# Two half buffers for the next layer's table, a group's later steps planned ahead of attention, and group buffers three deep

## The chip, the cores and the metric

The kernel runs on one core of a Trainium2 chip. Its time is the device time of one launch in microseconds (us). Three runs of the kernel before gave 5804.15, 5805.21 and 5806.6 us; their median, 5805.21 us, is the time before.

## The reference, cut to what matters

Two layers of a graph network with typed attention run over 6250 nodes of 128 values, 200,000 edges sorted by target node, 16 node types and 32 edge types; a linear map, the residual sum and a layer norm follow.

```python
def gt_layer(x, ntype, etype, src, dst, ...):          # H = 8 heads of 16, RT = 32 edge types
    k, q, v = (typed_linear(x, ntype, W) for W in (Wk, Wq, Wv))     # a matrix per node type
    kT = einsum('nhd,htdo->nhto', k, Watt)             # per node: 32 edge types x 128 values
    vT = einsum('nhd,htdo->nhto', v, Wmsg)
    a = einsum('ehd,ehd->eh', kT[src, :, etype], q[dst]) * pri[:, etype].T / sqrt(16)
    att = edge_softmax(a, dst, n)
    hag = segment_sum(vT[src, :, etype] * att, dst)
    h = silu(typed_linear(hag, ntype, Wa))
    h = h * alpha + x * (1 - alpha)                    # alpha: sigmoid(skip[ntype])
    return layernorm(h) * g + b
h = gt_layer(gt_layer(x, layer 0), layer 1)
out = layernorm(x + h @ ff_w + ff_b)
```

## The kernel before, in words

The nodes stand in 49 tiles of 128, ordered by their number of edges, so that a tile needs as many steps as its fullest node has edges, by a fixed table: 61 for the first tile, 45 for the next, down to 25, 24, 24 and 23 for the last four, 1613 in all. For each layer a table in DRAM holds, for each node and edge type, the row kT and vT (256 numbers, 1 KB). One step of a tile is one indirect DMA, issued by POOL (line 833), that gathers 128 such rows into a slot of the tile `ring` (64 slots in layer 0, 96 in layer 1).

There are three stages. First the edges are prepared and the table of layer 0 is written from x. Then layer 0 runs: POOL gathers, and VectorE (DVE) does attention over the slots (lines 854 to 888): scores, a softmax over the tile's steps, then the weighted values; a slot comes free only after its values are summed. Tiles form 15 groups, ten of four tiles and then groups of 3, 2, 2, 1 and 1. When a group's attention is done, `behind` takes it on: transposes of `hag` (line 384), sixteen masked matmuls with Wa (masks on DVE, line 937; matmuls, line 945), silu, the mixture with x, the norm; then `project` with another sixteen masks and three matmuls per mask for k, v and q of the next layer. A lock "m" lets one group at a time use these steps' PSUM banks; it is handed on when q is copied (line 952 or 954). Then `next_tables` computes, tile by tile, the rows of the next layer's table: 16 matmuls of 512 columns (line 442), each result copied by ScalarE (ACT) or DVE (line 451) into the staging tile `st`, 128 x 32 KB, and one indirect DMA of POOL (line 1049, 4 MB) that scatters `st` to the nodes' places. `st` is one buffer: a tile's copies wait for the landing of the tile before. Last comes layer 1: the same attention and `behind`, with `head` in place of `project`; its results are scattered to the output by line 1080.

The order of all instructions is made when the program is built, by a planner (`Plan`). Each step states its engine, its assumed duration and what it needs; the planner always takes the step that can start earliest, and among equals the one of the lower rank in RANK (attention 1, a group's later steps 3, table steps 0). Every engine then executes its list strictly in that order, so that an instruction that waits holds up all behind it on its engine. In the list a scatter stands MARGIN = 8 us behind the planned end of its copies, except in the last two groups. The planner knows nothing of a limit that the DMAs of POOL have in the trace.

Of the kernel before, what the change touches and what calls it, by code (L numbers as in the profile page):

```python
# [31 lines left out]
F32 = mybir.dt.float32  # L32
# [6 lines left out]
P = 128  # L39
# [21 lines left out]
RANK = dict(table=0, empty=0, gather=1, attend=1, prepare=2, mask=3, typed=3, late=4, query=1)  # L61
PLAN_US = None
GATHER_US = 1.31
# [36 lines left out]

class Clock:
# [24 lines left out]
class Plan:  # L126
# [3 lines left out]
    def __init__(self, us=0.0):  # L130
        self.free = {e: us for e in ("PE", "DVE", "ACT", "POOL", "SP", "DMA")}
        self.threads, self.born = [], 0
        self.clock = Clock()

# [12 lines left out]
    def start(self, t):  # L147
# [7 lines left out]
        if isinstance(took, Work):  # L155
            us = max(us, self.free["PE"])
            return None, us, "PE"
        names = engines if isinstance(engines, tuple) else (engines,)
# [3 lines left out]
    def run(self):  # L162
        while self.threads:
# [9 lines left out]
            if e == "PE":  # L173
                self.free[e], end, state = self.clock.run(us, t[4][1])
                self.clock.window, self.clock.busy, self.clock.full = state
            else:
                self.free[e] = end
            end += HOP_US
# [27 lines left out]
def gnn_kernel(ctx: ExitStack, tc: tile.TileContext, x, src, dst, etype, ntype, Wk, Wq, Wv, Wa,  # L206
# [221 lines left out]
    def table_rows(banks, st, kT, vT, j, bk, bv, needs, free):  # L428
# [3 lines left out]
        per = TAB // width  # L432
        halves = [[], []]
        for t0 in range(0, RT, per):
            i = 2 * t0 // RT
            filled = halves[i]
            for kv, (cT, blk) in enumerate(((kT, bk), (vT, bv))):
                for g in range(P // width):
# [10 lines left out]
                    def empty(to=st[:, t0 : t0 + per, c0 : c0 + width], tab=tab, done=done, us=us, i=i):  # L449
# [330 lines left out]
    def first_tables():  # L780
        free = [0.0, 0.0]
        for i, g in enumerate(GROUPS):
            yield "SP", 0.0, [made[i]]
            kT, vT = columns[i]
            for j, t in enumerate(g):
                dest = tables[0][t * P * RT : (t + 1) * P * RT].rearrange("(p t) c -> p t c", t=RT)
                halves = yield from table_rows(tabs, st, kT, vT, j, bk, bv, [made[i]], free)
# [39 lines left out]
    low = ctile("low", [P, NTILE, 2], I32)  # L827
    bp = ctx.enter_context(tc.tile_pool(name="bp", bufs=2))
# [99 lines left out]
    def typed_cols(fp, xm_bufs, xT, types, M, maps, needs):  # L928
# [11 lines left out]
        plan.spawn(mask(), RANK["mask"])  # L940
# [100 lines left out]
    def next_tables(i, kT, vT, bk, bv, us, at):  # L1041
        by_node = tables[1].rearrange("(n t) c -> n (t c)", t=RT)
        turn = locks["s"].take()
        for j, t in enumerate(LAST[i]):
            halves = yield from table_rows(tabs, at["rows"], kT, vT, j, bk, bv, [us, turn], [at["st"]] * 2)
            at["read"][i].us = plan.free["PE"] if j == len(LAST[i]) - 1 else None
            us = yield "SP", 0.0, halves[0] + halves[1]
            us = yield "POOL", GATHER_US, [us + (MARGIN if i + 2 < NG else 0.0)]
            s = nc.gpsimd.indirect_dma_start(
                out=by_node, out_offset=bass.IndirectOffsetOnAxis(ap=rec[:, t, 2:3], axis=0),  # L1050
                in_=at["rows"].rearrange("p t c -> p (t c)"), in_offset=None, bounds_check=NP - 1, oob_is_err=False)
            apart(s, "by_node")
            at["st"] = us + 16.0
        locks["s"].give(us - MARGIN)

    def head(fp, i, h, needs, at):
# [21 lines left out]
        for j, t in enumerate(g):  # L1078
            us = yield "POOL", GATHER_US, [us]
# [25 lines left out]
    def gathers(layer, ring, size, landed, freed):  # L1105
        for s in range(SLOTS):
            us = yield "POOL", GATHER_US, [freed[s - size]] if s >= size else []
# [4 lines left out]
    def attends(fp, layer, ring, pieces, st, weights, wa, landed, freed):  # L1112
        at = {c: [When() for _ in LAST] for c in ("hag", "h", "read", "out", "z", "ty")}
        at["st"], at["rows"] = 0.0, st
# [21 lines left out]
        for i, g in enumerate(LAST):  # L1136
            if i > 1:
                yield "SP", 0.0, [at["hag"][i - 2]]
            n = len(g)
            hag = fp.tile([P, GT, P], F32, tag="hag", name="hag", bufs=2)  # L1140
            for j, t in enumerate(g):
# [4 lines left out]
                if j == n - 1:  # L1146
                    got = yield "SP", 0.9, [at["ty"][i - 2]] if i > 1 else ()
                    xs = load4(fp, "xs", hid if layer else xperm, g[0], n, 2)
                    types = fp.tile([P, GT * P], F32, tag="types", name="types", bufs=2)
# [12 lines left out]
            plan.spawn(behind(fp, layer, i, hag, (xs, types, got + 3.0), [us], weights, wa, at), RANK["typed"], us)  # L1162

    for layer in range(L):
        last = layer == L - 1
        with tc.tile_pool(name=f"wp{layer}", bufs=1) as wp, tc.tile_pool(name=f"fp{layer}", bufs=1) as fp, \
# [8 lines left out]
            st = None if last else wp.tile([P, RT, ROW], F32, tag="st", name="st")  # L1175
# [136 lines left out]
```

## Time and profile before

| what | value |
|---|---|
| median of three runs | 5805.21 us |
| profiled execution | 5804.55 us, its span 5802.8 us |
| VectorE busy | 3647.5 us (63%) |
| POOL busy | 3589.4 us (62%), of it 3229.8 us in 3226 gathers |
| TensorE matmuls | 2683.0 us (46%), mean granted clock 0.674 |
| ScalarE busy | 908.2 us (16%) |

The span is the time from the first to the last instruction; the execution is 1.75 us longer. Times in the rows below count from the span's start. POOL's busy time covers the issue of a DMA, not its transfer.

### The profile page before, as it was taken

Reading aid. Unit: us, or ns where it says so; the run is one execution under the profiler, and the core shown is the slowest. Engines: PE = TensorE matmul, PEld = TensorE weight load, DVE = VectorE, ACT = ScalarE, POOL = GpSimd, SP = SyncE. Lnnn points to the kernel's source line nnn. Section 1 sums busy time; section 2 is a strip of 40 time slices with the busy share of each in tenths; the row PEclk is TensorE's granted clock in tenths of the full one; section 3 lists DMA queues with packets and bytes.
Section 4 is the critical chain, followed back from the end, with each engine's and each line's share of the span. In section 5 each row is a group of like instructions: output and inputs, shape, how many; then the busy total and the mean of one; then the engine's idle time right before and its main releaser. Section 6 shows DMA issues by size and latency. Waiting matters only on the chain. (4 is left out here: it accounts for less than half of the span.)

```text
span 5802.8 us, 36552 instructions
## 1 busy us (share of the span) xinstructions
PE 2683.0 (46%) x9472; PEld 1435.8 (25%) x9474; DVE 3647.5 (63%) x4965; ACT 908.2 (16%) x1768; POOL 3589.4 (62%) x3592
## 2 busy tenths in 40 slices
PE   5999998004656556676767785010111011111122
PEld 3666665002222222232223353000000000000011
DVE  5644453467667766676767551575676667766776
ACT  1333332001111121222212221000000000000001
POOL 2223511677777777767776602777777777777775
PEclk9999998556566667776677676555555555555555
DMA  7667766434545555555565534333333333333332
GB/s 207 244 247 271 280 237 265 107 102 133 183 161 188 181 185 174 194 190 189 189 209 193 193 129 155 107 109 102 106 109 108 102 106 110 108 108 107 106 108 71
DMA packets 331281, 924.13 MB, mean 159 GB/s; under 512 B 96992, under 2 KB 184412, under 8 KB 299704
## 3 DMA queue, kind: packets, MB, share of 16 engines
q0 software_dynamic: 172944, 649.13, 34.7%
q1 hardware_dynamic: 158120, 272.60, 13.2%
q8 instruction: 75, 1.23, 0.1%
q14 instruction: 142, 1.16, 0.1%
HBM read 485.42 MB, written 436.08 MB: 159 GB/s over the span
## 5 line engine op out<-in xcount | busy, mean ns | idle before, releaser
L833 POOL DMA_INDIRECT ring<-table,idx_all x3226 | 3229.8, 1001 | 1179.2 <-issue 997.3
L854 DVE TENSOR_TENSOR ring<-ring,sb 128x2048 f32<-128x2048 f32 (+13 forms) x261 | 453.8, 1739 | 889.9 <-DMA ring<-table,idx_all 877.3
L384 PE MATMUL xb<-ident,hag 128*128 128x128 f32 x98 | 39.8, 454 | 1826.0 <-DVE hag L1160 1824.0
L451 ACT COPY st<-tab 128x512 f32<-128x512 f32 x1165 | 628.1, 590 | 1198.6 <-PE tab L442 863.9
L885 DVE TENSOR_REDUCE add<-ring 128x128 f32<-128x2048 f32 (+13 forms) x269 | 735.5, 2734 | 9.1
L442 PE MATMUL tab<-bk,kT 32*128 32x512 f32 x1568 | 587.4, 784 | 330.9 <-ACT st L451 265.4
L442 PE MATMUL tab<-bv,vT 32*128 32x512 f32 x1568 | 577.4, 819 | 61.6 <-DVE st L451 34.2
L937 DVE SCALAR_TENSOR_TENSOR xm<-types,xb 128x512 f32<-128x512 f32 (+3 forms) x720 | 391.2, 584 | 241.8 <-PE aq L945 210.9
L945 PE MATMUL aq<-xm,wa 128*128 128x512 f32 (+3 forms) x960 | 448.0, 629 | 177.8 <-DVE xm L937 177.8
L856 DVE TENSOR_REDUCE sb<-ring 128x128 f32<-128x2048 f32 (+13 forms) x269 | 473.5, 1760 | 9.2
L384 PEld LDWEIGHTS xb<-ident,hag 128*128 128x128 f32 x98 | 17.9, 199 | 1861.0 <-DVE hag L1160 1842.5
L881 DVE TENSOR_TENSOR ring<-ring,sb 128x2048 f32<-128x2048 f32 (+13 forms) x269 | 469.4, 1745 | 0.0
L451 DVE COPY st<-tab 128x512 f32<-128x512 f32 x403 | 266.9, 686 | 218.7 <-PE tab L442 164.2
L1090 ACT COPY sb<-qr 128x128 f32<-128x128 f32 x96 | 25.9, 269 | 2099.7 <-DVE sb L856 1931.0
L945 PEld LDWEIGHTS aq<-xm,wa 128*128 128x128 f32 x960 | 208.4, 239 | 410.0 <-DVE xm L937 238.6
L397 DVE SCALAR_TENSOR_TENSOR xm<-types,xb 128x256 f32<-128x256 f32 (+1 forms) x400 | 157.5, 412 | 242.4 <-PE aq L414 241.2
L442 PEld LDWEIGHTS tab<-bk,kT 32*128 32x128 f32 x1568 | 183.4, 218 | 490.0 <-ACT st L451 359.5
L945 PE MATMUL ak<-xm,wk 128*128 128x512 f32 (+3 forms) x480 | 243.0, 591 | 107.2 <-DVE xm L937 107.1
L412 PE MATMUL kv<-xm,wk 128*128 128x256 f32 (+1 forms) x800 | 262.7, 410 | 9.2 <-DVE xm L397 9.2
L442 PEld LDWEIGHTS tab<-bv,vT 32*128 32x128 f32 x1568 | 193.5, 227 | 258.6 <-ACT st L451 162.5
L384 PE MATMUL xb<-ident,h 128*128 128x128 f32 x98 | 28.8, 437 | 493.6 <-DVE h L1011 493.6
L414 PEld LDWEIGHTS aq<-wq,xm 128*128 128x128 f32 x1568 | 238.7, 193 | 20.6
(176 smaller groups left out, 3105.1 us busy)
## 6 DMA issues: line engine op xcount, KB each, us to landing
table<-st SPq DMA_DIRECT2D x196, 1024.0 KB
ring<-table,idx_all POOLq DMA_INDIRECT x3226
state<-init SPq DMA_DIRECT2D x2, 3528.0 KB
state<-state SPq DMA_DIRECT2D x98, 72.0 KB
qr<-qrows SPq DMA_DIRECT2D x20, 256.0 KB
types<-tyrow SPq DMA_DIRECT2D x20, 256.0 KB
rows<-in_x_dram SPq DMA_DIRECT2D x24, 128.0 KB
types_i<-in_node_type_dram SPq DMA_DIRECT2D x24, 128.0 KB
```

Source lines behind the costliest of these rows:

```text
L397: nc.vector.scalar_tensor_tensor(xm, types[:, :M], float(t), xT[:, :M], op0=ALU.is_equal, op1=ALU.mult)
L412: nc.tensor.matmul(to, w[:, t], xm, start=False, stop=last_of)
L414: nc.tensor.matmul(to, xm[:, c], w[:, t], start=False, stop=last_of)
L442: nc.tensor.matmul(tab, cT[rows, nodes], blk[rows, t0 : t0 + per].rearrange("p t o -> p (t o)"), start=True, stop=True)
L451: (nc.scalar.copy if e == "ACT" else nc.vector.tensor_copy)(to, tab.rearrange("p (t o) -> p t o", o=width))
L833: nc.gpsimd.indirect_dma_start(out=ring[:, place], out_offset=None, in_=tables[layer], in_offset=bass.IndirectOffsetOnAxis(ap=idx[:, s : s ...
L854: nc.vector.tensor_tensor(kk, kk, q[:, None, :].to_broadcast([P, m, P]), op=ALU.mult)
L856: nc.vector.tensor_reduce(sc[:, s0 : s0 + m], kk.rearrange("p s (h d) -> p s h d", h=H), axis=AX.X, op=ALU.add)
L881: nc.vector.tensor_tensor(vv.rearrange("p s (h d) -> p s h d", h=H), vv.rearrange("p s (h d) -> p s h d", h=H), sc[:, s0 : s0 + m, :, None ...
L885: nc.vector.tensor_reduce(add, vv.rearrange("p s c -> p c s"), axis=AX.X, op=ALU.add)
L937: nc.vector.scalar_tensor_tensor(xm[:, :M], types[:, :M], float(t), xT[:, :M], op0=ALU.is_equal, op1=ALU.mult)
L945: nc.tensor.matmul(to[:, :M], w[:, t], xm[:, :M], start=(t == 0), stop=(t == NT - 1))
```

## The change

Four things change in the two layers; the preparation keeps its code.

`st` becomes two tiles of half the size, one for edge types 0 to 15 and one for 16 to 31. `next_tables` no longer waits with a tile for the landing of the one before: each half waits only for the scatter of the same half. Each half is scattered by a DMA of its own (`scatter`, 2 MB, POOL), by row numbers 2n and 2n + 1 in a new tile `half` (two small DVE instructions). The planner takes a half's landing to be 7.5 us after its issue, where it took 16 us for the whole.

The ranks change: a group's later steps get 1.2 and their masks 1.4, attention 1.6. Where both could start at once, the later steps now come first.

`hag`, `xs` and `types`, of which each group has one, are three deep, where they were two.

The planner gets a rule for POOL: a DMA may be issued only when the one issued eight before has landed (2.8 us for a gather, 8.0 us for a half scatter, as it assumes). A gather's issue is put at 1.303 us, where it was 1.31.

```diff
-RANK = dict(table=0, empty=0, gather=1, attend=1, prepare=2, mask=3, typed=3, late=4, query=1)
+RANK = dict(table=0, empty=0, gather=1, attend=1.6, prepare=2, mask=3, typed=3, late=4, query=1, behind=1.2, masks=1.4)
 PLAN_US = None
-GATHER_US = 1.31
+GATHER_US = 1.303
+LANES = 8
+LANDS_US = 2.8
+STORE_US = 8.0
...
+class Issue:
+    def __init__(self, us, lands):
+        self.us, self.lands = us, lands
...
+        if isinstance(took, Issue):
+            us = max(us, self.free["POOL"], self.lanes[-LANES])
+            return us + took.us, us, "POOL"
...
+                if isinstance(t[4][1], Issue):
+                    self.lanes.append(us + t[4][1].lands)
...
-                    def empty(to=st[:, t0 : t0 + per, c0 : c0 + width], tab=tab, done=done, us=us, i=i):
+                    def empty(to=st[i][:, :, c0 : c0 + width], tab=tab, done=done, us=us, i=i):
...
+    half = ctile("half", [P, NTILE, 2], I32)
+    for c in range(2):
+        nc.vector.tensor_scalar(half[:, :, c], rec[:, :, 2], 2.0, float(c), op0=ALU.mult, op1=ALU.add)
...
-        plan.spawn(mask(), RANK["mask"])
+        plan.spawn(mask(), RANK["masks"])
...
     def next_tables(i, kT, vT, bk, bv, us, at):
-        by_node = tables[1].rearrange("(n t) c -> n (t c)", t=RT)
         turn = locks["s"].take()
         for j, t in enumerate(LAST[i]):
-            halves = yield from table_rows(tabs, at["rows"], kT, vT, j, bk, bv, [us, turn], [at["st"]] * 2)
-            at["read"][i].us = plan.free["PE"] if j == len(LAST[i]) - 1 else None
-            us = yield "SP", 0.0, halves[0] + halves[1]
-            us = yield "POOL", GATHER_US, [us + (MARGIN if i + 2 < NG else 0.0)]
-            s = nc.gpsimd.indirect_dma_start(
-                out=by_node, out_offset=bass.IndirectOffsetOnAxis(ap=rec[:, t, 2:3], axis=0),
-                in_=at["rows"].rearrange("p t c -> p (t c)"), in_offset=None, bounds_check=NP - 1, oob_is_err=False)
-            apart(s, "by_node")
-            at["st"] = us + 16.0
-        locks["s"].give(us - MARGIN)
+            free, at["st"] = at["st"], [When(), When()]
+            halves = yield from table_rows(tabs, at["rows"], kT, vT, j, bk, bv, [us, turn], free)
+            for c in range(2):
+                plan.spawn(scatter(t, c, at["rows"][c], halves[c], at["st"][c], MARGIN if i + 2 < NG else 0.0, at),
+                           RANK["table"])
+        at["read"][i].us = plan.free["PE"]
+        locks["s"].give(plan.free["PE"])
+
+    def scatter(t, c, rows, filled, done, margin, at):
+        us = yield "SP", 0.0, filled
+        us = yield "POOL", Issue(GATHER_US, STORE_US), [us + margin]
+        s = nc.gpsimd.indirect_dma_start(
+            out=tables[1].rearrange("(n t) c -> n (t c)", t=RT // 2),
+            out_offset=bass.IndirectOffsetOnAxis(ap=half[:, t, c : c + 1], axis=0),
+            in_=rows.rearrange("p t c -> p (t c)"), in_offset=None, bounds_check=2 * NP - 1, oob_is_err=False)
+        apart(s, "by_node")
+        done.us = at["dma"] = max(us, at["dma"]) + 7.5
...
-            hag = fp.tile([P, GT, P], F32, tag="hag", name="hag", bufs=2)
+            hag = fp.tile([P, GT, P], F32, tag="hag", name="hag", bufs=3)
...
-            plan.spawn(behind(fp, layer, i, hag, (xs, types, got + 3.0), [us], weights, wa, at), RANK["typed"], us)
+            plan.spawn(behind(fp, layer, i, hag, (xs, types, got + 3.0), [us], weights, wa, at), RANK["behind"], us)
...
-            st = None if last else wp.tile([P, RT, ROW], F32, tag="st", name="st")
+            st = None if last else [wp.tile([P, RT // 2, ROW], F32, tag=f"st{c}", name=f"st{c}") for c in range(2)]
```

What this makes of the order is seen on two engines. POOL, layer 0, where the first scatters stand among the gathers, before (table_60 is the table of layer 0, table_61 that of layer 1):

```order
L833 DMA ring<-table_60,idx_all 128x256 x324
L1049 DMA table_61<-st,rec 6272x8192
L833 DMA ring<-table_60,idx_all 128x256 x30
L1049 DMA table_61<-st,rec 6272x8192
L833 DMA ring<-table_60,idx_all 128x256 x30
```

The same place now (st_6545 is the first half, st_6546 the second):

```order
L853 DMA ring<-table_60,idx_all 128x256 x286
L1075 DMA table_61<-st_6545,half 12544x4096
L853 DMA ring<-table_60,idx_all 128x256 x5
L1075 DMA table_61<-st_6546,half 12544x4096
L853 DMA ring<-table_60,idx_all 128x256 x12
```

The first scatter stands 38 gathers earlier, and the tiles of a group follow each other after 17 gathers and two scatters, where it was 30 gathers and one. POOL at the end of layer 0, before:

```order
L1049 DMA table_61<-st,rec 6272x8192
L833 DMA ring<-table_60,idx_all 128x256 x30
L1049 DMA table_61<-st,rec 6272x8192
L833 DMA ring<-table_60,idx_all 128x256 x8
L1049 DMA table_61<-st,rec 6272x8192 x9
L894 TENSOR_LOAD n_over
```

And now; of the ten scatters in a row at the end the first three are shown:

```order
L853 DMA ring<-table_60,idx_all 128x256 x4
L1075 DMA table_61<-st_6546,half 12544x4096
L853 DMA ring<-table_60,idx_all 128x256 x13
L1075 DMA table_61<-st_6545,half 12544x4096
L1075 DMA table_61<-st_6546,half 12544x4096
L1075 DMA table_61<-st_6545,half 12544x4096
```

Nine whole tiles stood behind the last gather, and 40 ahead of it; now five tiles (ten halves) stand behind it, and 88 halves ahead. DVE, layer 0, the ninth tile's softmax and first values (sb holds the scores, xm are masks of the group before, line 937), before:

```order
L865 TENSOR_TENSOR sb<-sb,top 128x312
L1006 SCALAR_TENSOR_TENSOR h<-h,al_87,xs 128x128 x2
L870 TENSOR_REDUCE den<-sb 128x8
L871 TENSOR_TENSOR state<-state,sb 128x8
L872 TENSOR_TENSOR den<-den,state 128x8
L873 TENSOR_TENSOR hag<-state,sb 128x128
L881 TENSOR_TENSOR ring<-ring,sb 128x16x128
L885 TENSOR_REDUCE add<-ring 128x128
```

The same place now:

```order
L885 TENSOR_TENSOR sb<-sb,top 128x312
L957 SCALAR_TENSOR_TENSOR xm<-types,xb 128x512 x4
L890 TENSOR_REDUCE den<-sb 128x8
L891 TENSOR_TENSOR state<-state,sb 128x8
L892 TENSOR_TENSOR den<-den,state 128x8
L893 TENSOR_TENSOR hag<-state,sb 128x128
L901 TENSOR_TENSOR ring<-ring,sb 128x16x128
L905 TENSOR_REDUCE add<-ring 128x128
L957 SCALAR_TENSOR_TENSOR xm<-types,xb 128x512 x2
L908 TENSOR_TENSOR hag<-hag,add 128x128
```

Masks of the projection, which stood behind this tile, now stand inside its attention, ahead of the sums that free ring slots.

## Rows read from the trace of the kernel before

**Rows 1.** Page: its head, its costliest group (busy, mean | idle).

```profile
span 5802.8 us, 36552 instructions
L833 POOL DMA_INDIRECT ring<-table,idx_all x3226 | 3229.8, 1001 | 1179.2 <-issue 997.3
```

**Rows 2.** Busy time by stage (instructions), granted clock, DMA share.

```profile
core 0: us, PE busy (x) PEld busy (x) DVE busy (x) ACT busy (x) POOL busy (x), PEclk, DMA share, GB/s
1001.34:3313.50 2312.16, 1277.07 (x2900) 543.43 (x2900) 1555.73 (x1855) 409.09 (x794) 1653.71 (x1653) 0.66 0.53 174
3313.50:3585.49 271.99, 216.72 (x784) 133.31 (x784) 112.31 (x242) 75.56 (x141) 9.74 (x11) 0.68 0.35 146
3585.49:5802.80 2217.31, 287.73 (x725) 150.76 (x725) 1489.57 (x1887) 124.82 (x259) 1665.05 (x1662) 0.54 0.36 105
```

**Rows 3.** Timeline, POOL, one scatter: start, us, instruction [idle, releaser].

```profile
1700.13 1.01 POOL L1049 DMA_INDIRECT table<-st,rec  x1 [0.30 <-issue]
1701.44 1.03 POOL L833 DMA_INDIRECT ring<-table,idx_all  x1 [0.30 <-issue]
...
1713.93 1.00 POOL L833 DMA_INDIRECT ring<-table,idx_all  x1 [3.63 <-DMA table<-st,rec]
1715.23 1.00 POOL L833 DMA_INDIRECT ring<-table,idx_all  x1 [0.31 <-issue]
```

**Rows 4.** Waits of POOL, 1001.34 to 3314: total, times, longest.

```profile
POOL ring L833 <- DMA table<-st,rec: 145.4, 39, 4.7
POOL ring L833 <- DVE add L885: 14.4, 4, 13.5
...
POOL table L1049 <- ACT st L451: 2.4, 2, 1.3
```

**Rows 5.** Groups by line, 1001.34 to 3313.5: busy, mean | idle.

```profile
L451 ACT COPY st<-tab 128x512 f32<-128x512 f32 x565 | 304.7, 589 | 587.3 <-PE tab L442 373.0 <-DMA table<-st,rec 213.6
...
L854 DVE TENSOR_TENSOR ring<-ring,sb 128x2048 f32<-128x2048 f32 (+14 forms) x129 | 220.3, 1708 | 369.4 <-DMA ring<-table,idx_all 365.7 <-DVE xm L937 0.8
```

**Rows 6.** Timeline, POOL, last gather of layer 0 to layer 1.

```profile
3313.50 0.99 POOL L833 DMA_INDIRECT ring<-table,idx_all  x1 [3.61 <-DMA table<-st,rec]
3328.48 1.01 POOL L1049 DMA_INDIRECT table<-st,rec  x1 [13.99 <-ACT st L451]
...
3457.67 0.96 POOL L1049 DMA_INDIRECT table<-st,rec  x1 [38.26 <-ACT st L451]
...
3568.75 0.96 POOL L1049 DMA_INDIRECT table<-st,rec  x1 [23.46 <-ACTq L896]
3585.49 1.05 POOL L833 DMA_INDIRECT ring<-table,idx_all  x1 [15.77 <-issue]
```

**Rows 7.** By stretch: the last scatter's transfer, the restart.

```profile
3570.35:3580.35 10.00, 0.00 (x0) 0.00 (x0) 0.00 (x0) 0.00 (x0) 0.00 (x0) 0.50 0.91 390
3580.35:3585.49 5.14, 0.00 (x0) 0.00 (x0) 0.00 (x0) 1.28 (x1) 0.01 (x1) 0.50 0.01 2
```

**Rows 8.** Timeline, DVE, end of the 47th tile's attention.

```profile
3274.08 0.29 DVE L1160 TENSOR_TENSOR hag<-hag,den 128x128 f32<-128x128 f32 x1
```

**Rows 9.** Timeline, TensorE, where two late groups take the lock.

```profile
3392.64 0.69 PE L384 MATMUL xb<-ident,hag 128*128 128x128 f32 x2 [0.46 <-ACT q L952]
...
3458.11 0.47 PE L384 MATMUL xb<-ident,hag 128*128 128x128 f32 x1 [0.46 <-ACT q L952]
```

**Rows 10.** Waits, 3313.5 to 3585.49: total, times, longest.

```profile
ACT st L451 <- DMA table<-st,rec: 110.2, 8, 29.4
```

**Rows 11.** Timeline, ScalarE, copies for the 47th and 48th tile.

```profile
3497.06 1.07 ACT L451 COPY st<-tab 128x512 f32<-128x512 f32 x2 [13.98 <-DMA table<-st,rec]
...
3524.80 0.58 ACT L451 COPY st<-tab 128x512 f32<-128x512 f32 x1 [6.38 <-DMA table<-st,rec]
```

**Rows 12.** Timeline, POOL, last gather and last output of layer 1.

```profile
5750.95 0.99 POOL L833 DMA_INDIRECT ring<-table,idx_all  x1 [0.30 <-issue]
...
5794.43 0.96 POOL L1080 DMA_INDIRECT out_dram<-o,rec  x1 [7.70 <-DVE o L976]
```

More of the change, by code (lines that the diff above doesn't have):

```diff
@@ L133, in __init__ @@
         self.clock = Clock()
+        self.lanes = [0.0] * LANES
     def spawn(self, steps, rank, us=0.0):
@@ L432, in table_rows @@
         per = TAB // width
+        assert 2 * per == RT
         halves = [[], []]
@@ L786, in first_tables @@
                 dest = tables[0][t * P * RT : (t + 1) * P * RT].rearrange("(p t) c -> p t c", t=RT)
-                halves = yield from table_rows(tabs, st, kT, vT, j, bk, bv, [made[i]], free)
+                halves = yield from table_rows(tabs, [st[:, : RT // 2], st[:, RT // 2 :]], kT, vT, j, bk, bv, [made[i]], free)
                 free = [When(), When()]
@@ L1078, in head @@
         for j, t in enumerate(g):
-            us = yield "POOL", GATHER_US, [us]
+            us = yield "POOL", Issue(GATHER_US, LANDS_US), [us]
             s = nc.gpsimd.indirect_dma_start(
@@ L1106, in gathers @@
         for s in range(SLOTS):
-            us = yield "POOL", GATHER_US, [freed[s - size]] if s >= size else []
+            us = yield "POOL", Issue(GATHER_US, LANDS_US), [freed[s - size]] if s >= size else []
             gather(layer, ring, idx_all, s, s % size)
@@ L1113, in attends @@
         at = {c: [When() for _ in LAST] for c in ("hag", "h", "read", "out", "z", "ty")}
-        at["st"], at["rows"] = 0.0, st
+        at["st"], at["rows"], at["dma"] = [0.0, 0.0], st, 0.0
         qs, ready, read = {}, [When() for _ in range(NTILE)], [When() for _ in range(NTILE)]
@@ L1136, in attends @@
         for i, g in enumerate(LAST):
-            if i > 1:
-                yield "SP", 0.0, [at["hag"][i - 2]]
+            if i > 2:
+                yield "SP", 0.0, [at["hag"][i - 3]]
             n = len(g)
-            hag = fp.tile([P, GT, P], F32, tag="hag", name="hag", bufs=2)
+            hag = fp.tile([P, GT, P], F32, tag="hag", name="hag", bufs=3)
             for j, t in enumerate(g):
@@ L1146, in attends @@
                 if j == n - 1:
-                    got = yield "SP", 0.9, [at["ty"][i - 2]] if i > 1 else ()
-                    xs = load4(fp, "xs", hid if layer else xperm, g[0], n, 2)
-                    types = fp.tile([P, GT * P], F32, tag="types", name="types", bufs=2)
+                    got = yield "SP", 0.9, [at["ty"][i - 3]] if i > 2 else ()
+                    xs = load4(fp, "xs", hid if layer else xperm, g[0], n, 3)
+                    types = fp.tile([P, GT * P], F32, tag="types", name="types", bufs=3)
                     nc.sync.dma_start(out=types[:, : n * P], in_=tyrow[ds(g[0] * P, n * P)][None, :].to_broadcast([P, n * P]))
```

## The prediction, made before the changed kernel was run

> **What bounds the kernel now.** I read the page first, then busy time by stage, then the waits and the timeline of POOL in layer 0, then the end of layer 0. The page shows no engine over 63% busy; the costliest group is POOL's gather, 3226 times [rows 1]. The span splits into a preparation up to 1001.3, the gathers of layer 0 (2312.2 us), the end of layer 0 without a gather (272.0) and layer 1 (2217.3) [rows 2]. In steady work one gather follows another after 1715.23 - 1713.93 = 1.30 us (1.303 over longer stretches) [rows 3], though one is busy for 1001 ns only [rows 1]. In layer 0 POOL issues 1613 gathers and 40 scatters up to the last gather, 1652 steps of 1.303 us = 2152.6 of the 2312.2 us. So issue by POOL bounds this stage; DVE is no bound, it stands 365.7 us before the scores waiting for gathers [rows 5].
>
> The other 159.6 us have two known causes. The first is a wait behind each scatter: seven gathers go out at the usual pace, and the eighth, due at 1710.6, starts at 1713.93, held until the scatter has landed [rows 3]. POOL's queue here takes eight DMAs in flight. 39 such waits are booked as 145.4 us [rows 4]; without the ordinary 0.30 us each they are 133.7, and a 40th of 3.8 us is booked on another line, so 137.5. The second is a wait of 13.1 us (13.45 less the ordinary gap; it is most of the 14.4) near the start, where the ring is full with the first tile [rows 4]. 9.0 us remain in small pieces.
>
> The end of layer 0 is the next place to look: 272 us in which POOL only issues the last nine scatters [rows 6]. ScalarE stands 110.2 us in it for the landing of a scatter before it may refill `st` [rows 10]. Layer 1 is bound by issue in the same way, but has no scatter of table rows: 1613 gathers and 45 output scatters by 1.303 us fill 2160 us of it up to the last gather [rows 2, 12].
>
> **The change, part by part.** The sum is made against the profiled execution, 5804.55 us, which is 0.66 us under the median of the three runs; its span is 5802.8 [rows 1], and 1.75 us lie around it.
>
> 1. Half scatters, the waits behind them. From issue to landing a scatter takes 13.7 us among gathers (the eighth gather starts 1713.93 - 1700.13 = 13.8 after it, less its own start) [rows 3], and 11.8 alone: of the 16.74 us from the last scatter to the restart, 5.1 belong to the restart [rows 6, 7]. Its transfer fills the DMA engines to 0.91 for 10.0 of those us [rows 7], so the time goes with the bytes. Half the bytes save 5: 8.7 us among gathers, 6.9 alone. The eighth DMA behind it is due after 8 x 1.303 = 10.4 us, so it no longer waits: -137.5 us. The bounds are 0 wait, and 3.4 us for each half if the landing didn't shrink.
>
> The Trainium skill, "DMA: Bandwidth & Descriptors", section "Anatomy of one DMA — SWDGE (gpsimd) path", puts a DMA of this kind at about 2.0 us plus its bytes by 436 GB/s, and its section "Rules for kernel authors" advises to join transfers into few large ones, which speaks against splitting. By that fit a whole scatter is 11.6 us, which the trace bears out with 11.8, and a half 6.8; the second fixed part, 49 x 2.0 = 98 us, would come on top if it stood on the path. Here POOL goes on issuing in that time, so I don't charge it.
>
> 2. Half scatters, the issue. 98 take the place of 49. By the order 88 stand ahead of the last gather where 40 stood: 48 x 1.303 = +62.5 us, all on the path, since POOL is the bound there.
>
> 3. POOL waits for its own scatters' data. Before, 40 scatters waited 2.4 us in all [rows 4]. But their copies had more room: the gathers ran late by 3.4 us per tile against the list, and the list reckoned with 16 us of landing where 13.7 were needed. Now both cushions are gone and 8 us of margin stay. The bounds are 0 and, if every half came 3 us late, 264 us; I take 20 (one half in ten late by 2 us), near the small end, because that is the row there is.
>
> 4. Ranks. The order shows six masks of the projection and a norm's steps now standing between a tile's scores and its first freed slots. No row gives one such mask alone; at the price of ScalarE's copy of as many columns, 589 ns [rows 5], six are 3.5 us, and I add as much for the norm: 7 us. Before, the first slot came free some 17 us after the tile's last gather: the first tile leaves 3 of 64 slots, 3.9 us of gathers, and then POOL waits 13.1 [rows 4]. With 7 more it is 24. From the fifth tile on a tile has 40 slots or fewer, so 24 or more are free then, 31 us of gathers. So no new ring wait: 0, and up to 10 us for each of ten groups if the masks themselves are late, since they stand in line for TensorE.
>
> 5. Deeper `hag`, `xs`, `types`, and the `half` instructions: 0. Nothing on POOL's path waits for them; two DVE instructions on 49 numbers stand beside loads at the change of stage.
>
> So the gathers of layer 0 take 1700 x 1.303 + 13.1 + 9.0 + 20 = 2257.2 instead of 2312.2, and the last one starts at 1001.3 + 2257.2 = 3258.5 instead of 3313.5. Call that time T.
>
> 6. The end of layer 0. Before, the order held nine tiles' rows back behind the last gather, now five. What ends it is the chain of the last groups through the lock. The 47th tile's attention ended at 3274.4 [rows 8], 31 us after its last gather (47 gathers, two scatters and two waits of 3.4 before 3313.5, that is 3243). Now 47 gathers and 5 halves lie between that gather and T, 67.8 us, so it ends at T - 36. Its group held the lock for 3458.1 - 3392.6 = 65.5 us [rows 9], in which, as an estimate, one refill's wait for a landing stood, 110.2 / 8 = 13.8 us [rows 10]; 52 remain, so the lock is free at T + 16. The last two groups, one tile each, took 3585.5 - 3458.1 = 127.4 us from there to layer 1 [rows 6, 9]. Of these go: 12 us of the 13.98 that ScalarE stood for a landing ahead of the 47th tile's rows, since its first half was sent some 7 us earlier and lands sooner; the 6.38 before the 48th's [rows 11]; and 4.9 of the last landing. 104 stay. Layer 1 starts at T + 120 = 3378.5 instead of 3585.5. What is late next is the chain itself: masks, norm, projection, copies of one group after the other. The bounds: 95, if the other waits for `st` go too, and 160, if the table rows of four tiles crowd into the chain on TensorE.
>
> 7. Layer 1. The same gathers and the same 45 outputs ahead of the last one. After the last gather come 43.5 us to the last output's issue [rows 12]; now the last group but one has its steps and its output ahead of the last tile's values: -4 us (bounds +5 and -10).
>
> The preparation's list is made anew with 1.303 for 1.31; it ends with the landing of the last table rows. I take 0 and keep 10 us either way.
>
> Sum: 5804.55 - 207.0 - 4 = 5593.5, so 5594 us. Its own range, from 0 to 90 us in part 3, 95 to 145 in part 6 and the small ones, is 5550 to 5650.
>
> **The rivals.** (a) POOL waits for table rows or for ring slots far more than before. For it speaks that the list has lost its cushions, and that one late matmul holds up masks, these hold up attention, and attention the ring; against it that DVE has 365.7 us of idle time before its scores [rows 5]. At 2 us per half it costs 176 instead of 20: 5750 us.
>
> (b) The waits behind the scatters go, but the end of layer 0 is not shortened, because the chain of groups ends as late behind the last gather as now. Then only -137.5 + 62.5 + 20 - 5 remain of layer 0, -60, with layer 1 5741 us. Against it: ScalarE's 110.2 us for landings [rows 10].
>
> (c) The slower side: a half takes nearly as long to land as a whole, by cost per row and not per byte (each still writes 128 places). Then every eighth DMA behind a half waits, and halves sent 5 gathers apart queue up. At 3.4 us by 88 it is +299 against -137.5, with the issue and 20 us +244 in the gathers; the end gains 121 (five tiles left in place of nine): 5804.55 + 123 - 4 = 5924 us. It turns into a loss where a half lands later than about 12.8 us after its issue (10.4 + 211/88), against 8.7 expected; the 10.0 us of full transfer speak against it [rows 7].
>
> **How the numbers follow.** The forecast has 0.70, (a) 0.14, (b) 0.07, (c) 0.04; 0.03 go to a better end than its own range, 0.02 to no effect, by a worse preparation or chain. The range for 8 in 10 is 5545 to 5740: it reaches over (a) up to its middle and to the edge of (b); outside lie 0.03 below, and above it (c), no effect, and about half of (a) and (b), 0.16. Faster by over 0.2% (11.6 us, about what a measurement here tells from no change) are the forecast, the better end, (b), and (a) unless its waits pass 220 us: 0.92. Within 0.2%: 0.02. Slower: (c) and the worst of (a), 0.06.
>
> **What would show it.** POOL's waits for the landing of `st` scatters gone, with the gathers' stage near 2257 us; about 88 scatters in it, each followed by the next gather after 1.30 us; POOL's waits for table copies near 20 us in all; ring waits only near the start; the end of layer 0 near 120 us; layer 1 at 2213. It is wrong if the eighth DMA behind a half still waits, if POOL stands more than 90 us for copies or slots, or if the end of layer 0 stays over 150 us.

## The result, and the profile after

Four runs of the changed kernel gave 5645.3 to 5655.74 us, median 5648.65; four of the kernel before beside them 5804.73. The ratio is 0.973 (95% interval 0.9719 to 0.9743). The prediction said 5594, with 5545 to 5740 as its range. The profiled execution took 5649.23 us. All medians and ratios leave out one run, of e3, at a lower granted clock (6951 us at 0.562; the nine others 6481 to 6522 us at 0.65 and above). By stage (columns as in [rows 2]; the first line is the preparation, then the gathers of layer 0, its end, layer 1):

```profile
core 0: us, PE busy (x) PEld busy (x) DVE busy (x) ACT busy (x) POOL busy (x), PEclk, DMA share, GB/s
0.00:1023.52 1023.52, 910.60 (x5061) 616.89 (x5065) 491.15 (x983) 298.55 (x577) 263.26 (x269) 0.97 0.66 243
1023.52:3292.76 2269.24, 1394.12 (x3185) 614.87 (x3186) 1584.56 (x1945) 453.80 (x871) 1704.44 (x1700) 0.66 0.56 185
3292.76:3440.95 148.19, 129.16 (x500) 76.77 (x499) 57.03 (x138) 40.97 (x76) 10.72 (x11) 0.74 0.35 147
3440.95:5647.47 2206.52, 279.92 (x725) 148.13 (x725) 1480.99 (x1887) 127.69 (x261) 1665.62 (x1662) 0.55 0.36 105
```

| stage | before | predicted | after |
|---|---|---|---|
| preparation | 1001.3 | 1001.3 (± 10) | 1023.5 |
| gathers of layer 0 | 2312.2 | 2257.2 | 2269.2 |
| end of layer 0 | 272.0 | 120 | 148.2 |
| layer 1 | 2217.3 | 2213 | 2206.5 |

The waits behind the scatters [rows 3, 4] are gone: behind none of the 88 halves does the eighth DMA start later than the ordinary gap allows. POOL around two halves of one tile (start, us, instruction, idle and releaser):

```profile
1700.29 1.01 POOL L1075 DMA_INDIRECT table<-st,half  x1 [0.30 <-issue]
...
1708.14 1.01 POOL L1075 DMA_INDIRECT table<-st,half  x1 [0.30 <-issue]
...
1710.79 1.00 POOL L853 DMA_INDIRECT ring<-table,idx_all  x1 [0.31 <-issue]
```

The eighth DMA behind the first half starts at 1710.79, 10.5 us after it, with the ordinary gap of 0.31. POOL's longest waits in this stage, beside the ordinary gaps (508.0 us over 1575 gathers), and last its only line for a scatter's landing:

```profile
POOL table L1075 <- ACT st L468: 26.6, 16, 5.9
POOL table L1075 <- issue: 24.1, 69, 3.4
POOL ring L853 <- DVE add L905: 14.0, 3, 13.4
POOL table L1075 <- ACT sb L1116: 9.1, 2, 8.8
...
POOL ring L853 <- DMA table<-st,half: 0.3, 1, 0.3
```

The last line is one ordinary gap. The other lines too hold the ordinary gap of 0.30 for each issue; beyond it POOL stands 33.2 us ahead of its half scatters (21.6 for copies, 8.5 once behind a copy of q, 3.1 without a named cause).

### The profile page after: what moved, and what is told of

Its sections match the earlier page's. It is cut to its first block, busy times and chain, and to the rows that moved or that the text cites. A ratio compares the mean times of both kernels' runs of the same rounds, so it can differ in the third digit from the quotient of the medians.

```text
span 5647.5 us, 36732 instructions
## 1 busy us (share of the span) xinstructions
PE 2713.8 (48%) x9470; PEld 1456.7 (26%) x9474; DVE 3613.7 (64%) x4952; ACT 921.0 (16%) x1785; POOL 3644.0 (65%) x3641
## 5 line engine op out<-in xcount | busy, mean ns | idle before, releaser
L459 PE MATMUL tab<-bk,kT 32*128 32x512 f32 x1568 | 704.1, 833 | 280.9 <-ACT st L468 248.7
L459 PE MATMUL tab<-bv,vT 32*128 32x512 f32 x1568 | 600.5, 837 | 27.0 <-ACT st L468 14.6
L965 PE MATMUL aq<-xm,wa 128*128 128x512 f32 (+3 forms) x960 | 438.5, 618 | 68.3 <-DVE xm L957 67.8
L459 PEld LDWEIGHTS tab<-bk,kT 32*128 32x128 f32 x1568 | 215.8, 231 | 507.4 <-ACT st L468 423.6
L820 POOL DMA_INDIRECT qrows<-qall,posn x49 | 48.2, 984 | 344.3 <-ACT qall L791 184.0
L430 PE MATMUL aq<-wq,xm 128*128 128x128 f32 x1568 | 241.8, 276 | 0.0
```

Of the source, the lines that this page charges most:

```text
L430: nc.tensor.matmul(to, xm[:, c], w[:, t], start=False, stop=last_of)
L459: nc.tensor.matmul(tab, cT[rows, nodes], blk[rows, t0 : t0 + per].rearrange("p t o -> p (t o)"), start=True, stop=True)
L965: nc.tensor.matmul(to[:, :M], w[:, t], xm[:, :M], start=(t == 0), stop=(t == NT - 1))
```

## The experiments

The kernels that are called mended differ from the changed one in two things, which the first two runs take apart. The runs fell on three chips: e1 to e4 on one where the kernel before takes 6499 us (25 runs), e5 to e8 on one where it takes 6566 (13 runs), e9 to e12 on one where it takes 5804.56 (9 runs), as in the first measurement. Stages are therefore compared inside a chip (the chip of the first measurement is called the first chip); what the chips of e1 to e8 do is told in the last section. Stage times are those of the profiled executions, ratios go against the kernel before on the same chip.

**The preparation: e1 and e2.** In the changed kernel the two instructions for `half` stand in the preparation, as the timeline of DVE shows; the prediction missed it. They wait there:

```profile
454.19 0.42 DVE L413 SCALAR_TENSOR_TENSOR xm<-types,xb 128x256 f32<-128x256 f32 x1 [0.73 <-PE aq L430]
472.75 0.31 DVE L847 TENSOR_SCALAR half<-rec 128x49 int32<-128x49 int32 x2 [18.14 <-DMA rec<-recs]
```

In the kernel before the first reader of `rec` stood later and waited 7.0 us (waits of DVE):

```profile
DVE deg_p L611 <- DMA rec<-recs: 7.0, 1, 7.0
```

Run e1 moves the two instructions behind that reader:

```diff
...
         nc.vector.tensor_copy(ty, rec[:, :, 3])
+        for c in range(2):
+            nc.vector.tensor_scalar(half[:, :, c], rec[:, :, 2], 2.0, float(c), op0=ALU.mult, op1=ALU.add)
...
-    for c in range(2):
-        nc.vector.tensor_scalar(half[:, :, c], rec[:, :, 2], 2.0, float(c), op0=ALU.mult, op1=ALU.add)
```

> The changed kernel; only the two DVE instructions that make `half` are moved: in the preparation they now stand right behind the two casts of `rec` (where DVE waits for `rec` anyway) and not ten instructions ahead of them. Theory P: of the 22.2 us that the preparation lost, about 11 come from these two instructions, which held DVE for 18.1 us until `rec` had landed, and 11 from the list that was made anew with 1.303 us. It expects the first gather of layer 0 at 1012 us (1023.5 in the changed kernel) and 5638 us in all. Rival P1: the new list alone is the cause, the wait only fills time that DVE has: first gather at 1023, 5649 us. Rival P2: the wait alone is the cause: first gather at 1002, 5627 us. The other stages stay within 3 us in all three.

Run e2 plans the preparation with 1.31 us as well:

```diff
+FIRST_US = 1.31
...
-            us = yield "POOL", n * GATHER_US, [us, *seen[-2:][:1]]
+            us = yield "POOL", n * FIRST_US, [us, *seen[-2:][:1]]
...
-            us = yield "POOL", GATHER_US, ()
+            us = yield "POOL", FIRST_US, ()
...
-                yield "POOL", GATHER_US, [placed, queried[i]]
+                yield "POOL", FIRST_US, [placed, queried[i]]
```

> As the kernel before it (`half` behind the casts), and the preparation is planned with 1.31 us per POOL issue as before the change, the layers with 1.303. Theory P expects the whole loss of the preparation back: first gather at 1001 to 1003 us, 5627 us in all. Rival P3: the preparation's time differs from launch to launch or by where code and tiles lie, and the lists are no cause: it stays at 1012 or above. The layers' stages stay at 2269 (gathers), 148 (end of layer 0) and 2207 us (layer 1), each within 4 us.

Measured: first gather at 1087.0 (e1) and 1055.5 us (e2), 1052.1 in e3, whose preparation is that of before. The expected absolute times don't hold on this chip, but the difference counts: the list alone, 1.303 for 1.31, makes the preparation 31.4 us longer in this pair of profiles. So rival P2 (the wait alone) falls; P1 (the list alone) isn't excluded. Ratios: e1 1.0005 (0.9982 to 1.0028), e2 0.996 (0.9936 to 0.9985).

**The same on a chip as in the first measurement: e10 and e11** (five runs each; e10 is the changed kernel, e11 the kernel of e2).

> The changed kernel as it is, beside the mended one on the same chip. Theory P: its first gather comes 22 us later than the mended one's on a chip where the kernel before takes 5805 us, and 40 to 45 us later on one like those so far (there the list alone cost 31 us between the first two runs, and the two instructions of `half` about 11 more); the layers are the same within 10 us. Rival P1 (the wait for `rec` only fills time that DVE has): 31 us or less there.

> The mended kernel (list of the preparation planned with 1.31 us, `half` behind the casts). Theory P: 22 us faster than the changed one where the kernel before takes 5805 us (5627 us), 40 to 45 us faster on a chip like those so far. Rival: no difference in total, since the layers give it back.

Measured: e10 5653.35 us, ratio 0.9737 (0.9723 to 0.975); e11 5632.22 us, 0.9704 (0.9688 to 0.972): 21.1 us faster, the best of all kernels here beside e12. Their first gathers:

```profile
1029.26 1.05 POOL L853 DMA_INDIRECT ring<-table,idx_all  x1 [27.90 <-issue]
```

```profile
1008.32 1.05 POOL L854 DMA_INDIRECT ring<-table,idx_all  x1 [27.49 <-issue]
```

20.9 us in one pair of profiles, 21.1 in the medians; the layers agree within 3 us. So list and wait together are the loss of the preparation, and rival P3 falls. The split into two equal parts, which theory P made, isn't borne out: on the chip of e1 to e4 the list alone gave 31.4 us, not 11. The share of the wait was measured nowhere by itself. e9, the kernel before, starts at 1002.99 on this chip; the 5 us to e11 stay open (e12, with the same preparation, starts at 1005.92).

**Whole scatters with the new ranks and depth: e3.** The kernel before with `RANK` and the three deep buffers of the changed one.

> The kernel before with the new ranks and the three deep buffers, but with one staging tile and one whole scatter per tile, and the planner as before (1.31 us, 16 us of landing, no rule for eight). Theory H (the halves do the work: they remove the waits behind the scatters and the waits of the copies for the landing): the eighth POOL DMA behind each of 41 scatters still waits 3.4 us, the gathers of layer 0 take 2305 to 2320 us, the end of layer 0 with eight tiles behind the last gather 240 to 265 us, layer 1 2207 us, 5765 us in all. Rival R (the ranks shorten the end of layer 0, since a group's later steps start sooner): the end of layer 0 falls to 170 us or less, 5690 us or less in all.

Measured: 6503.4 us, ratio 0.9994 (0.998 to 1.0008); end of layer 0 261.1 us with eight tiles behind the last gather:

```profile
3751.04:4012.15 261.11, 202.73 (x729) 121.23 (x728) 83.38 (x195) 67.32 (x123) 8.79 (x10) 0.69 0.32 133
```

Theory H holds for this stage, R falls: with whole scatters the new ranks and the depth take 11 of the 272 us, which are from a chip of the other kind. The waits behind the scatters are there:

```profile
POOL ring L833 <- DMA table<-st,rec: 140.0, 39, 4.7
```

The gathers' stage (2698.9) and the total are not comparable with the expected ones on this chip. Inside the chip they say something that the first measurement doesn't: with halves the gathers take 2758.3 us (e2), 59 more. The waits of POOL behind scatters are gone there, but those for ring slots are 214.4 us in place of 91.6, and 47 issues are added; e2 gains at the end of layer 0 alone, 148.3 against 261.1.

**The halves alone: e4, and again e6.** The ranks of before, groups two deep.

```diff
-RANK = dict(table=0, empty=0, gather=1, attend=1.6, prepare=2, ...
+RANK = dict(table=0, empty=0, gather=1, attend=1, prepare=2, ...
...
-        plan.spawn(mask(), RANK["masks"])
+        plan.spawn(mask(), RANK["mask"])
...
-            hag = fp.tile([P, GT, P], F32, tag="hag", name="hag", bufs=3)
+            hag = fp.tile([P, GT, P], F32, tag="hag", name="hag", bufs=2)
...
```

> The halves alone: half buffers, half scatters and the planner's rule for POOL, with the ranks of the kernel before (attention 1, later steps 3), group buffers two deep, and the preparation mended as in the kernel of run two. The order has 84 halves ahead of the last gather and 14 behind it (88 and 10 in the changed kernel). Theory H: no waits behind scatters; gathers of layer 0 (1612 + 84) x 1.303 + 22 + 20 to 40 = 2252 to 2272 us, end of layer 0 150 to 180 us (seven tiles' rows instead of five, no waits for landings), layer 1 2217 us, 5630 to 5665 us in all. Rival R: without the ranks the groups' steps come late, the end of layer 0 stays above 220 us, 5700 us or more.

> The kernel of e4_half_only again, for the same reason. On the chip of the first four runs its end of layer 0 took 219 us, between the two theories. Theory R2 (the ranks give about half of what the end of layer 0 gained, the halves the rest): gathers of layer 0 2250 to 2270 us, end 205 to 235 us, layer 1 2217 us, 5690 us in all. Theory H (the halves alone give it): end 180 us or less, 5650 us or less.

Measured: 6570.26 and 6597.58 us, ratios 1.0105 (1.0084 to 1.0126) and 1.0052 (1.0035 to 1.0068). End of layer 0, e6 and then e5 (the mended kernel on the same chip):

```profile
3822.78:4041.08 218.30, 186.32 (x704) 109.92 (x704) 98.76 (x212) 60.10 (x113) 14.57 (x16) 0.75 0.35 142
```

```profile
3816.63:3972.74 156.11, 137.06 (x501) 80.58 (x500) 56.69 (x138) 41.10 (x76) 10.74 (x12) 0.71 0.34 139
```

H (180 or less) falls. In e4 the stage lies just under R's 220 us, and in e6 inside R2's range: with the old ranks seven tiles' rows stand behind the last gather where five do with the new ones, and the stage takes 62 to 71 us more (219.3 against 148.3 in e4 and e2). Against the 272 us before, the halves alone take 53, the ranks alone 11 (e3), both 124: each needs the other. (The 272 are from a chip of the other kind; but e2 has the changed kernel's 148 there too.) Over all runs the end goes with the number of tiles whose rows the order leaves behind the last gather: four 114.2 us (e8), five 148.2 to 156.1, seven 190.1 (e7) to 219.3, eight 261.1 (e3), nine 272.0 and 273.7 (e9). So halves and ranks act at least in part by letting the planner send more tiles ahead of it; how much comes of that alone, no run shows. Behind none of the half scatters does POOL wait for a landing, with the old ranks as with the new. The totals say little of the first measurement, since on these chips layer 1 too is 50 us longer with the old ranks than with the new; but there the halves alone are slower than the kernel before. The planner's rule for eight DMAs and its 1.303 us in the layers came with the halves in every run, and nothing takes them apart.

**The mended kernel again: e5.**

> The kernel of e2_both again (the first four runs were on a chip where the kernel before takes 6499 us, so that they can be compared only with each other). On a chip where the kernel before takes 5805 us, theory P expects the first gather at 1001 to 1003 us where the changed kernel has 1023.5, and 5627 us in all, since list and wait of `half` make up the 22.2 us; rival P3 (they are not the cause): 1012 us or later, 5638 us or more. The layers: 2269, 148 and 2207 us, each within 4.

Measured: again a chip where neither theory's absolute times apply; 6505.23 us, ratio 0.992 (0.9901 to 0.9938), with an end of layer 0 of 156.1 us where e2 has 148.3; the cause of these 8 us is open. It is the base for the next two.

**Both halves one behind the other: e7.** A tile's halves are sent when both are filled.

```diff
-            for c in range(2):
-                plan.spawn(scatter(t, c, at["rows"][c], halves[c], at["st"][c], MARGIN if i + 2 < NG else 0.0, at),
+            plan.spawn(scatter(t, at["rows"], halves[0] + halves[1], at["st"], MARGIN if i + 2 < NG else 0.0, at),
...
```

> The mended kernel, but both halves of a tile are scattered one right behind the other, when both are filled; so the same bytes are under way at once as with one whole scatter, in two DMAs. Theory L (POOL takes eight DMAs in flight, and the eighth waits if the bytes ahead have not landed by then): the eighth DMA behind a pair waits again, 2 to 3.4 us for each of 42 pairs, 85 to 140 us; gathers of layer 0 2340 to 2405 us, end 160 to 200 us (seven tiles behind the last gather). Rival S (a half simply has a shorter way through the queue, whatever is beside it): no such waits, gathers of layer 0 2255 to 2275 us.

Measured: 6551.45 us, 0.9977 (0.9962 to 0.9992). That is 46 us over e5; in the profiles the gathers take 26 more and the end, with seven tiles behind the last gather, 34 more. Neither size holds: POOL's waits that are booked on a landing are ten, 9.5 us beyond the ordinary gap. But each stands at the eighth DMA behind the second half of a pair, and nine of them (9.2 us) where the pair is 2.6 us apart:

```profile
1819.43 1.01 POOL L1077 DMA_INDIRECT table<-st,half  x1 [0.30 <-issue]
...
1822.07 1.00 POOL L1077 DMA_INDIRECT table<-st,half  x1 [0.31 <-issue]
1823.38 1.03 POOL L854 DMA_INDIRECT ring<-table,idx_all  x1 [0.30 <-issue]
...
1831.22 0.99 POOL L854 DMA_INDIRECT ring<-table,idx_all  x1 [0.30 <-issue]
1833.53 0.99 POOL L854 DMA_INDIRECT ring<-table,idx_all  x1 [1.31 <-DMA table<-st,half]
```

12 of the 42 pairs are that close; in the others POOL waited for the second half's copies and they lie 3.7 to 14.3 us apart. In the three close pairs that are not among the nine the eighth waits too, 1.4 to 2.0 us, without a named cause. The second half shown is waited for until 1833.53 - 1822.07 = 11.5 us after its issue, 1.0 us over the usual place of the eighth; a whole scatter 13.8, 3.3 over it [rows 3]; a single half never. That bears out theory L's mechanism (the eighth waits for the landing), with a landing that I took too late, and rival S, by which no such wait comes, falls.

**Quarters: e8.** Each half by two DMAs of 1 MB.

```diff
+        for k in (2 * c, 2 * c + 1):
+            us = yield "POOL", Issue(GATHER_US, STORE_US), [us + margin]
...
+                out=tables[1].rearrange("(n t) c -> n (t c)", t=RT // 4),
```

> The mended kernel, but each half is scattered by two DMAs of 1 MB, one right behind the other; the buffers and the copies stay halves. The order has 180 scatters ahead of the last gather (88 with halves) and 16 behind it (four tiles). Theory I (in this stage every DMA that POOL issues costs 1.303 us of the path, and waits hide behind it): 92 more cost 120 us, gathers of layer 0 2375 to 2400 us, end of layer 0 135 to 150 us, 90 to 120 us over the mended kernel in all. Rival (smaller pieces land sooner, so that copies and POOL's waits for them gain, or the issue lies beside waits that POOL has anyway): less than 70 us over the mended kernel.

Measured: 6642.17 us, ratio 1.0115 (1.0087 to 1.0142), 137 us over e5. Gathers of layer 0:

```profile
1059.39:4012.61 2953.22, 1586.46 (x3261) 654.64 (x3262) 1590.60 (x1956) 463.39 (x883) 1802.34 (x1792) 0.62 0.44 143
```

193.9 us more than e5's 2759.36, of which 92 issues by 1.303 are 119.9. The rival (under 70) falls: POOL's busy time alone grew by 94.5 us, and it isn't won back in POOL's waits, which grew as well. The other 74 come with longer waits for ring slots (255.7 against 197.1) and copies (349.2 against 324.0); why these grew was not tried. Theory I's price of an issue fits, its sizes don't: 137 us lie above its 90 to 120, and the end, 114.2 us with four tiles, below its 135 to 150.

**Without the depth: e12.**

> The mended kernel with `hag`, `xs` and `types` two deep again: halves and ranks without the depth. POOL's order is the same as the mended kernel's. Theory D0 (the depth gives nothing, the ranks and halves do it all): every stage as in the mended kernel, within 10 us. Rival D1 (the depth is what lets a group's steps start early): end of layer 0 60 us longer and layer 1 50 us longer, as with the halves alone.

Measured: 5629.8 us (5626.82 to 5647.87), ratio 0.9695 (0.968 to 0.971), as e11. End of layer 0 148.7 and layer 1 2208.5 us (e11: 148.2 and 2209.2). Its profiled run was its longest and has 14 us more in the gathers of layer 0, beyond D0's 10; its other three runs (5626.8 to 5631.7) are 16 us shorter and have no profile. In the total and in the two stages that D1 names D0 holds, and D1 falls: beside halves and ranks the depth brings nothing.

**The kernel before: e9.**

> The kernel before, to have its stages on a chip like those of the runs so far, where TensorE's masked matmuls with Wa come some 5.6 us apart after a pause and a group's copy of their sum starts up to 47 us late. Theory C (there the chain of a group's steps, not POOL's issue, sets much of the time, and what the change does for it decides): preparation 1052 us (as in the kernel with the whole scatter), gathers of layer 0 2590 to 2660 us with 135 us of waits behind scatters, end of layer 0 280 to 330 us, layer 1 2550 us (as with the halves alone, which has the old ranks too). Rival: the stages all grow by one factor (6499/5805 = 1.12): preparation 1121, gathers 2589, end 305, layer 1 2483 us. On a chip where this kernel takes 5805 us: the stages shown for it, each within 5 us.

Measured: 5807.34 us, first gather 1003.0, gathers 2312.3, end 273.7, layer 1 2216.5: the stages shown for it, as expected for such a chip. Theory C was therefore not tested.

## Why the prediction was right in kind and 55 us too low

The forecast was 5593.5. The four stages differ from it by +22.2, +12.0, +28.2 and -6.8: 55.6, which is the profiled 5649.2.

*Parts 1 and 2, right.* No wait stands behind any of 88 halves, and 1700 steps of 1.303 us are as reckoned; e3 brings the waits back with whole scatters, e7 in part, and e8's issues cost what part 2 says. One reading goes too far: that POOL's queue takes eight DMAs in flight. In the trace POOL's DMAs use eight semaphores in turn, and each of the 40 DMAs that were held carries a wait for the very semaphore that it uses itself, which the scatter eight before it raises when it lands. So the eight belong to the program as it is built; how many the queue would take, no run shows. The half's way from issue to its buffer's refill, put at 8.7 us, was 1683.30 - 1675.45 = 7.85 where ScalarE stood for it (7.8 to 9.0 over the 56 such waits of ScalarE and DVE). Issue and copy:

```profile
1675.45 1.01 POOL L1075 DMA_INDIRECT table<-st,half  x1 [0.30 <-issue]
```

```profile
1683.30 1.07 ACT L468 COPY st<-tab 128x512 f32<-128x512 f32 x2 [9.99 <-DMA table<-st,half]
```

Rival (c), cost per row and not per byte, is refuted by this. The Trainium skill's fit for such a DMA, on its page "DMA: Bandwidth & Descriptors", section "Anatomy of one DMA — SWDGE (gpsimd) path", gives, as an estimate, 6.8 us for a half alone; among gathers the trace has 7.85. The Trainium skill's advice in the same page's section "Rules for kernel authors", to join many small transfers into one large one, names sizes under 64 KB, which no run here has. Quarters of 1 MB lose in e8; halves of 2 MB win on the first chip, together with the new ranks, since what holds POOL there is the wait at the eighth DMA and not the transfers' sum.

*Part 3, mis-sized.* 33.2 us for 20. All but one wait (5.6 us at 2826) stand from 3129 us on, from the 39th tile; before that the 8 us of margin hold.

*Part 4, right.* The ring waits stay at 13.1 us.

*Part 5 and the preparation, wrong.* "Two DVE instructions on 49 numbers stand beside loads at the change of stage" is not what the order says: they stand some 530 us earlier, in the preparation; and the list made anew was put at 0 ± 10. Together they cost 22.2, past that bound (21 in e10 against e11).

*Part 6, mis-sized by 28.* The stage begins 34 us later than forecast for the reasons above, and is 148.2 long. The prediction took 13.8 us of a landing out of the time for which a group of two holds the lock. But TensorE was busy for 58.96 of these 65.47 us in the kernel before (24.4 of them with table matmuls), so that with the same matmuls in the hold at most 6.5 could go (the hold, then the last two groups):

```profile
3392.64:3458.11 65.47, 58.96 (x200) 36.99 (x201) 38.11 (x70) 18.68 (x36) 2.37 (x3) 0.76 0.33 136
3458.11:3585.49 127.38, 93.64 (x392) 59.95 (x392) 36.22 (x108) 33.37 (x61) 4.37 (x6) 0.66 0.40 168
```

The same two stretches after:

```profile
3243.70:3322.30 78.60, 68.31 (x206) 36.96 (x206) 52.14 (x91) 22.59 (x44) 34.04 (x34) 0.72 0.54 192
3322.30:3440.95 118.65, 99.91 (x381) 57.12 (x380) 37.53 (x106) 33.42 (x62) 7.67 (x8) 0.69 0.35 145
```

The hold is now 78.6 us where 52 were forecast, with 68.3 of TensorE's, among them 29.4 of table matmuls of earlier tiles. It begins 49 us ahead of the last gather where 36 were forecast, so that it ends 13.5 us late; the last two groups take 118.7 where 104 were forecast: TensorE's idle time fell there from 33.7 to 18.7, but its busy time grew by 6.3. This is the crowding that the bound of 160 us had named. ScalarE's 110.2 us for landings [rows 10] are gone to the last, where the sum had taken off 32 of them (13.8, 12 and 6.4); its longest line in the stage is now a wait for TensorE, which is busy for 129.2 of the 148.2 us:

```profile
ACT st L468 <- PE tab L459: 63.7, 32, 8.0
```

That the ranks were needed for it (e4, e6) was no term of the prediction.

*Part 7, mis-sized.* The gathers of layer 1 take 2166 us as before, to 0.5; the end behind them is 40.6 us instead of 51.8. The first of the last outputs before [rows 12]:

```profile
5780.65 1.00 POOL L1080 DMA_INDIRECT out_dram<-o,rec  x1 [28.70 <-DVE xm L937]
```

The last outputs now:

```profile
5606.92 0.99 POOL L853 DMA_INDIRECT ring<-table,idx_all  x1 [0.30 <-issue]
5624.35 1.00 POOL L1106 DMA_INDIRECT out_dram<-o,rec  x1 [16.44 <-DVE o L996]
...
5643.73 0.97 POOL L1106 DMA_INDIRECT out_dram<-o,rec  x1 [13.34 <-DVE o L996]
```

The first of them comes 17.4 us behind the last gather, where it was 29.7, so the steps of the groups before the last come earlier, as the prediction had it: -11 in place of -4, past the bound of -10 by 1.

Rival (b) is refuted on this chip by 148 against 272 us, rival (a) by 33 us; on the chips of e1 to e8 POOL does stand as in (a), though with whole scatters too (e3: 249.3 us for copies and 91.6 for slots). The end of layer 0 stays only 2 us under the 150 us that the prediction named as a sign of being wrong.

## What to carry to other kernels

Where one engine issues many small DMAs and a few large ones, look for waits at a fixed number of DMAs behind a large one: a smaller piece that lands before its queue place comes round removes the wait, for the price of one more issue, and a still smaller one only costs; whether the total gains is read from the waits that come in its place. Before a wait is taken out of a chain, compare the busy time of the next engine with the length of the stretch: no more than the idle rest can go, unless that engine's work moves out too. A new instruction, and a planner's constant, may act in a stage that the change doesn't name; read the order of that stage too.

## What the runs showed of the hardware

On the chips of e1 to e8 TensorE is done with its masked matmuls far later than their records in the trace say. It is seen on DVE, which may make the next mask of 512 columns only when TensorE has raised its semaphore for an earlier one. First group of layer 0, e5:

```profile
1361.53 0.69 DVE L958 SCALAR_TENSOR_TENSOR xm<-types,xb 128x512 f32<-128x512 f32 x1 [4.91 <-remote]
1367.13 0.69 DVE L958 SCALAR_TENSOR_TENSOR xm<-types,xb 128x512 f32<-128x512 f32 x1 [4.91 <-remote]
```

The changed kernel on the first chip:

```profile
1322.04 0.69 DVE L957 SCALAR_TENSOR_TENSOR xm<-types,xb 128x512 f32<-128x512 f32 x1 [0.17 <-PE aq L965]
1322.89 0.69 DVE L957 SCALAR_TENSOR_TENSOR xm<-types,xb 128x512 f32<-128x512 f32 x1 [0.17 <-PE aq L965]
```

A mask comes every 5.60 us instead of 0.86. The timeline calls the releaser in e5 "remote", but the semaphore that DVE waits for is TensorE's, and in the trace it is raised every 5.60 us too (1355.90, 1361.51, 1367.11). The granted clock (PEclk, the third number from the end; 1.00 is 2.4 GHz and 0.50 is 1.2) is not the same in the two places, e5 first:

```profile
1358.00:1361.00 3.00, 0.30 (x1) 0.00 (x0) 0.00 (x0) 0.00 (x0) 2.37 (x3) 1.00 0.30 87
1367.00:1373.00 6.00, 2.08 (x2) 0.50 (x2) 0.96 (x2) 0.00 (x0) 3.28 (x4) 0.50 0.23 66
```

```profile
1318.00:1327.00 9.00, 9.00 (x22) 3.81 (x21) 7.16 (x11) 0.00 (x0) 6.86 (x8) 0.98 0.34 99
```

But the clock isn't the whole difference: the step of 5.60 us stands at either level in e5, while the first chip has 1.70 us at 0.50 (the semaphore at 1315.28 and 1316.98) and 0.86 at 1.00. Over layer 1 the mean clocks are nearly alike, 0.54 and 0.55. The recorded durations of the matmuls, 0.59 to 1.22 us, don't show it. In layer 1 of e5 a group's copy of the sum starts 47 us behind the end of the last recorded matmul of the sum. It isn't so everywhere on these chips: the end of layer 0, where TensorE is busy for most of the time, takes 148.3 us in e2 and 148.2 on the first chip. Where it is so, a group's steps are late, and POOL waits for copies and slots in layer 0, in e5:

```profile
POOL table L1076 <- ACT st L470: 324.0, 37, 40.3
POOL ring L854 <- DVE add L906: 197.1, 14, 28.2
```

26.6 and 14.0 us are the same waits on the first chip. So the gain differs by chip: 3% with the mended kernel where the kernel before takes 5805 us, 0.4% and 0.8% on the two others. That TensorE's pace is the cause of this fits the waits, but no run shows it by itself, and what causes the pace stays open.
